# Written order on four engines for the three chains of attention units, and one load on another engine's queue

## The chip, the cores and the metric

The kernel is one launch on one core of a Trainium2 chip. The time is the device time of that launch in microseconds; three runs are shown with their median. One more execution was taken with the hardware profiler on, and everything that is read from a trace comes from it. Engines are named as in the profile: PE is TensorE (PEld its weight loads), DVE is VectorE, ACT is ScalarE, POOL is GpSimd, SP is SyncE, which issues most of the DMAs.

## The reference, cut to what matters

The program is a decoder of four layers on `x`, 4 sequences of 256 tokens of width 128, with a second input `ctx`, 4 sequences of 512 keys. Layers 0, 1 and 3 have multi-head attention with 16 heads of 8; in outline:

```python
# layer 0
x = x + self_attention(norm(x))                    # 16 heads of 8, keys are x's own 256 rows
x = x + cross_attention(norm(x), norm(ctx), mask)  # 512 keys, with a key mask
x = x + moe(norm(x))                               # 32 experts, best 1, and a shared expert
# layer 1
x = x + causal_self_attention(norm(x))
x = x + strided_cross_attention(norm(x), norm(ctx))  # keys are every 16th row of ctx
x = x + moe(norm(x))                               # 8 experts, best 2
# layer 2: linear attention, latent attention, moe
# layer 3
x = x + latent_self_attention(norm(x))             # queries and keys through a narrow product
x = x + cross_attention(norm(x), ctx)              # 512 keys, an additive mask
x = x + quantised_ffn(norm(x))                     # rows rounded to integer steps, GELU, rounded again
```

Each normalisation is a layer norm over 128 columns. The router of a mixture takes the logits of the normalised rows, chooses the experts, and computes for each token its rank within its expert.

## The kernel before, in words

**Units.** `woven` runs the attention of one layer as a chain of *units*. A unit is one sequence in one kind of attention: layer 0 has units 0 to 3 (self, 256 keys) and 4 to 7 (cross, 512 keys), layer 1 has four, layer 3 has units 0 to 3 (latent) and 4 to 7 (cross). A unit is made of small steps:

- its *prelude*: `norm` (statistics on VectorE, L309; then on GpSimd `ve` L314, a power, and the normalised rows, `xn` or `xq`, L322), `source` (the rows turned by TensorE, L332, evicted as `xnT`, L292), in layer 3's first half the latent product (L941), then `queries` (L463 to L503) and `keys` (L512 to L526). In units 0 and 1 queries and keys stay on the chip; from unit 2 on in layers 0 and 3 each is split into three bf16 parts, written to DRAM (`qp`, `kp`) and read back in another arrangement (L497, L526) by DMAs on SP's queue. In layer 0 these land in a part of the tile `e0h` that is lent to them; in layer 3 in `cn`, `w2kv`, `kk` and `qq`.
- *beats*: half of a group of row scores (L564 or L582, with the row maximum on VectorE, L571 or L575) and half of a group of column scores (L643, L656 or L679, with the exponential on ScalarE, L673). Row maxima of one unit are made while the columns of the unit before are. The PSUM ring of scores has 7 buffers; one beat takes 4.
- *late* steps: `weighted` (L701, eight matmuls for half a group), `divided_by_sums`, `transposed_result`, `added`, and after them `u.after`, a list of further steps spread over `u.within` of a unit. In layer 0's units 4 to 7 and in all of layer 1 that list ends with the router's steps (in layer 1 the strided attention's stand ahead of them); in layer 3's units 4 to 7 it is the quantised feed-forward (`quantised_steps`): `norm`, `quantise` (its first instruction is the reduction `am`, L2154), `turn`, `hidden` (two products, then GELU on ScalarE, L2187), `quantise_hidden` (L2154 again), two `turn_hidden`, `result`.
- *beside*: steps of other work that are spread over the unit. In layer 0's units 0 to 3 these are the means and scales of the context; in unit 0 a fourth one is `loads`, the first half of layer 0's expert weights (`e0h`, four DMAs of 1 MB, L2282).

**The written order.** Every step carries a place within the unit, as a fraction. `back` gives the beats and late steps, `front` the preludes of units n + 1, n + 2 and n + 3 and the steps beside; `run` sorts by the fraction and calls them. What lies at 1.0 or later is carried into the next unit.

**What sets the order of execution.** The framework keeps each instruction's data dependencies. Where the code isn't inside `tc.manual_schedule`, its planner chooses the order of the instructions on every engine, by its own idea of when each could start. Two other loops of the kernel (the expert blocks of layer 0's mixture, and the linear attention) run inside `tc.manual_schedule` already: there the engines named keep the order in which the code issues. `woven` did not. [...]DMAs are issued in order of the queue of the engine that issues them; here these are SP, ACT and, for the gathers, POOL.

At layer 3's start the tokens of layer 2's mixture are still being fetched: `back` (L1372, an indirect DMA on POOL's queue), and VectorE adds them to `x` (L1384) ahead of each unit's `norm`. Layer 3's constant parts of the keys and queries (`restk`, `restq`, L463) are written into DRAM early, during layer 0.

Of the kernel before, what the change touches and what calls it, by code (L numbers as in the profile page):

```python
# [203 lines left out]
def decoder(ctx: ExitStack, tc: tile.TileContext, dr, out):  # L204
    nc = tc.nc
    V, A, G, T = nc.vector, nc.scalar, nc.gpsimd, nc.tensor
# [79 lines left out]
    turn = [0]  # L286
# [9 lines left out]
    def normalise(srcs, dsts, on=None):  # L296

        scaled_by(statistics(srcs), srcs, dsts, on)
# [94 lines left out]
    def spread(fns, start, end):  # L393

        n = len(fns)
        return [(start + (end - start) * (i + 0.5) / n, f) for i, f in enumerate(fns)]

    def call(f, *args):
        return lambda *more: f(*args, *more)
# [32 lines left out]
    def woven(pool, units, n_keys, split=None, lent=None):  # L432
# [312 lines left out]
        def prelude(u):  # L745
            return [call(f, u) for f in u.prelude] + [call(queries, u), call(keys, u)]

        def groups_of_rows(u):
            if u.clip:
                return []  # L750
            return [call(rows_of, u, qt, g) for qt in range(2) for g in range(0, 4, 512 // u.nk)]
# [19 lines left out]
        def halved(groups):  # L771
            return [(f, h) for f in groups for h in range(2)]
# [22 lines left out]
        LEAD = 2  # L795
# [53 lines left out]
        def run(items):  # L849
            for _, f in sorted(items, key=lambda i: i[0]):  # L850
                f()
# [1 line left out]
        for n, u in enumerate(units):  # L853
            u.n, u.split = n, bool(split) and n > 1
        halves_of_rows = [halved(groups_of_rows(u)) for u in units]
        for f in prelude(units[0]) + [call(values, units[0])]:
            f()
        first = []
        if len(units) > 1:
            first += spread(prelude(units[1]), 0.0, 0.8)  # L860
        first += beats([], halves_of_rows[0] + halves_of_rows[1][:LEAD], units[0])[0]
        run(first)
        carried = []
        for n in range(len(units)):
            own, late = back(n)
            items = own + front(n) + carried + late
            run([i for i in items if i[0] < 1.0])
            following = 1.0
            if n + 1 < len(units):
                following = units[n].nkt / units[n + 1].nkt  # L870
            carried = [((at - 1.0) * following, f) for at, f in items if at >= 1.0]
        run(carried)

    def scaled(pool, bias):
        t = pool.tile([P, 1], F32, tag="qb", name="qb", bufs=2)
# [110 lines left out]
            spare.pop(0)(tag)  # L986

    class Router:  # L990

# [15 lines left out]
        def steps(r, pool, b, tag):  # L1007
            n_e, k = r.n_e, r.k
            mine = slice(2 * k * b, 2 * k * (b + 1))
            u = {}  # L1010
# [93 lines left out]
                else:  # L1104
                    V.tensor_copy(r.seen, total)

            out = [norm, turn, logits]
            if r.probs:
                out.append(softmax)
            out.append(choose)  # L1110
# [1033 lines left out]
    def quantised_steps(pool, b):  # L2144


        wq, ws = wq3
        u = {}

        def quantised(src, m, tag):  # L2150


            am = small.tile([P, 2], F32, tag="am", name="am")
            V.tensor_reduce(am, src, AX.X, ALU.max, apply_absolute_value=True)  # L2154
            V.tensor_scalar(am, am, EPS, None, ALU.max)
            sc = small.tile([P, 2], F32, tag="qs", name="qs")
            V.reciprocal(sc, am)
            V.tensor_scalar(sc, sc, 127.0, None, ALU.mult)
            un = small.tile([P, 2], F32, tag="un", name="un")
            V.reciprocal(un, sc)  # L2160
            V.tensor_scalar(un, un, ws[:, m : m + 1], None, ALU.mult)
            q = pool.tile(list(src.shape), F32, tag=tag, name=tag)
            for i in range(2):
                V.tensor_scalar(q[:, i], src[:, i], sc[:, i : i + 1], MAGIC, ALU.mult, ALU.add)
            V.tensor_scalar(q, q, MAGIC + 127.0, MAGIC - 128.0, ALU.min, ALU.max)
            return q, un

        def norm():
            two = [x[2 * b], x[2 * b + 1]]
            u["xn"] = pool.tile([P, 2, D], F32, tag="xq", name="xq")  # L2170
            normalise(two, [u["xn"][:, i] for i in range(2)], G)

        def quantise():
            u["q"], u["un"] = quantised(u["xn"], 0, "q1")

        def turn():
            u["qT"] = pool.tile([P, S], BF16, tag="qT1", name="qT1")
            transposed(
                [u["q"][:, i] for i in range(2)], u["qT"],
                lambda d, s: V.tensor_scalar(d, s, MAGIC, None, ALU.subtract), tag="s1",  # L2180
            )

        def hidden():
            hp = [product(u["qT"][:, i * P : (i + 1) * P], wq[0], "s1") for i in range(2)]
            u["h"] = pool.tile([P, 2, 512], F32, tag="h", name="h")
            for i in range(2):
                A.activation(u["h"][:, i], hp[i], AF.Gelu, scale=u["un"][:, i : i + 1])  # L2187

        def quantise_hidden():
            u["qh"], u["unh"] = quantised(u["h"], 1, "q4")  # L2190
            u["qhT"] = pool.tile([P, 2, 512], BF16, tag="qT4", name="qT4")

        def turn_hidden(i):
            transposed(
                [u["qh"][:, i, c * P : (c + 1) * P] for c in range(4)], u["qhT"][:, i],
                lambda d, s: A.activation(d, s, AF.Copy, bias=-MAGIC), tag="s1",
            )

        def result():
            y = ps("s1")  # L2200
            for i in range(2):
                for c in range(4):
                    T.matmul(
                        y[:, i * P : (i + 1) * P], lhsT=u["qhT"][:, i, c * P : (c + 1) * P],
                        rhs=wq[1][:, c * P : (c + 1) * P], start=c == 0, stop=c == 3,
                    )
            for i in range(2):
                t = 2 * b + i
                V.scalar_tensor_tensor(
                    x[t], y[:, i * P : (i + 1) * P], u["unh"][:, i : i + 1], x[t], ALU.mult, ALU.add  # L2210
                )
                nc.sync.dma_start(out[t * P : (t + 1) * P, :], x[t])

        return [
            norm, quantise, turn, hidden, quantise_hidden, call(turn_hidden, 0),
            call(turn_hidden, 1), result,
        ]

# [51 lines left out]
    def layer_0(wh, router):  # L2270
        with ExitStack() as st:
            st.enter_context(psum_pool("ps0"))
            pool = attn_pool(st, "l0")


            lent = Lent(wh[:, 16 * 512 :])
            neg0, neg0T = key_mask(pool, "mbk0", False, lent)

            def loads():
                for i in range(0, 16, 4):  # L2280
                    cols = slice(i * 512, (i + 4) * 512)
                    nc.sync.dma_start(wh[:, cols], dr["e0h"][:, cols])  # L2282

            units = self_units(pool, w0a, True, False, 0)
            units += cross_units(
                pool, w0x, 2, context_T,
                row_mask=lambda b: neg0[:, b * SK : (b + 1) * SK],
                key_bias=lambda b: lambda kt: neg0T[:, NKT * b + kt : NKT * b + kt + 1],
            )
            for u in units[:B]:  # L2290
                u.beside = [call(context_means, u.b, 0), call(context_means, u.b, 2)]
                u.beside += [call(context_scales, u.b)]
            units[0].beside += [loads]
            for u in units[B:]:
                u.beside = [call(normalise_context, u.b, i) for i in range(0, NKT, 2)]
                u.after, u.within = router.steps(pool, u.b, "s1"), 1.0
            woven(pool, units, SK, "l0", lent)
# [17 lines left out]
    def layer_3():  # L2315
        with ExitStack() as st:
            st.enter_context(psum_pool("ps3"))
            pool = attn_pool(st, "l3")
            mc, mcT = (added_mask(pool, k, 2, True) for k in ("mcau", "mcauT"))
            mf, mfT = added_mask(pool, "mif1", 2, False), added_mask(pool, "mif1T", NKT, False)  # L2320
            units = low_rank_units(
                pool, w3a, rows_mask=lambda qt: mc[:, qt, :], cols_mask=lambda kt: mcT[:, kt, :]
            )
            units += cross_units(
                pool, w3x, 10, lambda b: None, rows_mask=lambda b: lambda qt: mf[:, qt, :],
                cols_mask=lambda b: lambda kt: mfT[:, kt, :],
            )
            for u in units[B:]:
                u.after, u.within = quantised_steps(pool, u.b), 0.8
            lent = Lent(cn.rearrange("p t d -> p (t d)"), held["w2kv"])  # L2330
            woven(pool, units, SK, "l3", lent)

    with early:
        e0h = e0.tile([P, 32 * 512], F32, tag="e0h", name="e0h")
# [4 lines left out]
    late = ctx.enter_context(tc.tile_pool(name="late", bufs=1, reuse_waits="tile"))  # L2339
# [39 lines left out]
```

## Time and profile before

| what | value |
|---|---|
| three runs | 1522.98, 1516.32, 1518.51 us; median 1518.51 |
| profiled execution | 1517.87 us |
| its span | 1516.0 us, mean granted TensorE clock 0.912 |
| layer 0's attention | 7 to 282 us of the span |
| layer 1's attention | 336 to 472 |
| layer 3 | 1180 to 1516 |
| DMA | 95.85 MB, mean 63 GB/s |

A row of waits reads: engine, tile and line that waited, `<-`, what it waited for, then total us, number of times, longest one. A row of the timeline reads: start, duration, engine, line, operation, output and input, shapes, and in brackets how long the engine had been idle just before, and what ended that. `SPq` is SP issuing a DMA; the duration is that of the issue. In the page, a digit of the row PEclk is the granted TensorE clock in tenths for one fortieth of the span.

Layer 2, the mixtures and the loads between (282 to 336, 472 to 1180) are not part of `woven`.

### The profile page before, as it was taken

The page shows a single profiled execution, that of the slowest core. Times are in us where ns is not written, and L with a number is a line of the kernel's source. Part 1 is how long each engine was busy: PE and PEld are TensorE (multiplying, and loading weights), DVE is VectorE, ACT ScalarE, POOL GpSimd, SP SyncE. Part 2 cuts the span into 40 slices and gives each one's busy share as a digit, 9 for nine tenths or more (in the row PEclk, how much of TensorE's full clock was granted, in tenths as well). Part 3 has the DMA queues.
Part 4 walks back from the last instruction along what each step waited for, and adds up shares of the span by engine and source line. Part 5 has one row for each costly group of instructions (what it writes and reads, how often), then busy time and mean ns, then how long its engine had stood idle before and what let it go on. Part 6 is the DMA issues. An engine that isn't in the chain of part 4 may idle for free.

```text
span 1516.0 us, 29457 instructions
## 1 busy us (share of the span) xinstructions
PE 1292.0 (85%) x11200; PEld 709.5 (47%) x11200; DVE 821.6 (54%) x2696; ACT 722.7 (48%) x1462; POOL 324.1 (21%) x481
## 2 busy tenths in 40 slices
PE   4878999796787998879999999999597489898894
PEld 2434454343354664535555555555365244443442
DVE  6368785485654346555445445452333456776643
ACT  0343667285542334257767757756121024345464
POOL 6133221344123316000000000000331613322000
PEclk9699999896897999999999999999698579999997
DMA  3432120620132115230111000000312112221000
GB/s 137 171 101 89 62 66 6 239 55 14 62 157 87 41 34 208 83 120 15 56 46 43 1 5 1 1 4 1 128 39 56 35 50 78 95 62 62 6 5 8
DMA packets 50873, 95.85 MB, mean 63 GB/s; under 512 B 6881, under 2 KB 31947, under 8 KB 49067
## 3 DMA queue, kind: packets, MB, share of 16 engines
q1 hardware_dynamic: 46318, 77.61, 14.8%
q0 software_dynamic: 3264, 6.69, 2.0%
q10 hardware_dynamic: 1152, 9.67, 1.6%
q8 instruction: 90, 1.47, 0.4%
q14 instruction: 49, 0.40, 0.1%
HBM read 66.20 MB, written 29.72 MB: 63 GB/s over the span
## 4 chain that ended last, share of the span: by engine, by line
PE 62%; DVE 10%; ACT 8%; DMA 7%; POOL 7%; issue 5%; SPq 1%; ACTq 0%; POOLq 0%; DVEq 0%
PE o L2040 6%; PE g L1299 6%; PE o L701 5%; PE s L2020 5%; PE f L1966 4%; PE s L582 4%; PE y L1323 3%; PE s L679 3%; PE f L1952 2%; PE s L643 2%; DMA e0h<-kp 2%; DVE mx L571 2%; PE s L656 2%; PE t L1308 2%; PE s L2013 2%
## 5 line engine op out<-in xcount | busy, mean ns | idle before, releaser
L673 ACT ACTIVATE pr<-s 128x512 f32<-128x512 f32 x384 | 206.4, 597 | 254.1 <-PE s L679 160.4
L314 POOL TENSOR_SCALAR ve<-mv 128x2 f32<-128x2 f32 x44 | 10.7, 243 | 743.6 <-DVE mv L309 738.6
L1977 ACT ACTIVATE ss<-ss,ntop 128x768 f32<-128x768 f32 x128 | 118.6, 928 | 91.1 <-DVE ntop L1975 90.9
L571 DVE TENSOR_REDUCE mx<-s 128x1 f32<-128x512 f32 (+1 forms) x192 | 122.5, 684 | 61.8 <-PE s L656 25.3
L701 PE MATMUL o<-pr,v 128*32 128x256 f32 (+1 forms) x1792 | 146.2, 396 | 7.5 <-ACT os L707 6.0
L1971 DVE CUSTOM_DVE_ANT_0 ss<-f,n 128x512 f32<-128x512 f32 x128 | 83.5, 689 | 68.7 <-PE f L1966 68.7
L2040 PE MATMUL o<-pr,v 128*64 128x256 f32 x768 | 107.5, 395 | 1.0 <-ACT pr L2027 0.9
L575 DVE CUSTOM_DVE_ANT_0 junk<-s,nmif 128x512 bf16<-128x512 f32 x128 | 82.9, 688 | 36.0 <-PE s L679 35.5
L2020 PE MATMUL s<-qT,kT 64*128 64x256 f32 x768 | 101.5, 381 | 0.0
L2027 ACT ACTIVATE pr<-s,n 128x512 f32<-128x512 f32 x128 | 80.3, 678 | 24.4 <-PE s L2020 24.2
L582 PE MATMUL s<-e0h 32*128 32x512 bf16 (+1 forms) x576 | 73.0, 365 | 18.8 <-DMA e0h<-kp 18.3
L1277 POOL DMA_INDIRECT xb<-sent,token x62 | 60.0, 968 | 105.7 <-PE t L1284 59.0
L1966 PE MATMUL f<-kT,qT 64*128 64x512 f32 x256 | 78.1, 629 | 2.2 <-ACT kT L294 1.1
L1959 DVE CUSTOM_DVE_ANT_0 ss<-f,nought 128x256 f32<-128x256 f32 x128 | 46.7, 421 | 54.6 <-PE f L1952 53.1
L2040 PEld LDWEIGHTS o<-pr,v 128*64 128x64 f32 x768 | 47.8, 137 | 57.3 <-issue 22.7
L701 PEld LDWEIGHTS o<-pr,v 128*32 128x32 f32 x1792 | 40.1, 110 | 70.6 <-issue 46.4
L679 PE MATMUL s<-e0h 32*128 32x256 bf16 x960 | 68.4, 273 | 3.6 <-DVE mx L571 2.2
L2020 PEld LDWEIGHTS s<-qT,kT 64*128 64x128 f32 x768 | 67.8, 190 | 6.0
L656 PE MATMUL s<-qm,kc 32*128 32x512 f32 (+1 forms) x256 | 64.3, 710 | 0.0
L575 DVE CUSTOM_DVE_ANT_0 junk<-s,nmcau 128x256 bf16<-128x256 f32 x128 | 46.2, 421 | 32.9 <-PE s L656 15.0
L332 PE MATMUL s<-consts,xn 128*128 128x128 f32 x64 | 20.2, 371 | 46.0 <-POOL xn L322 46.0
L322 POOL TENSOR_SCALAR xn<-x,mv,rs 128x128 f32<-128x128 f32 x72 | 56.8, 797 | 3.8
(482 smaller groups left out, 2663.2 us busy)
## 6 DMA issues: line engine op xcount, KB each, us to landing
qp<-qp SPq DMA_DIRECT2D x36, 192.0 KB, 2.3
kd<-ahead SPq DMA_DIRECT2D x20, 256.0 KB, 2.6
vd<-ahead SPq DMA_DIRECT2D x20, 256.0 KB
kT<-kd SPq DMA_DIRECT2D x20, 256.0 KB, 4.9
v<-vd SPq DMA_DIRECT2D x5, 1024.0 KB, 5.3
e0h<-qp SPq DMA_DIRECT2D x6, 768.0 KB
e0h<-in_e0h SPq DMA_DIRECT2D x4, 1024.0 KB, 12.0
e0h<-in_e0h SPq DMA_DIRECT2D x1, 4096.0 KB
```

What stands on the lines that cost most here:

```text
L571: V.tensor_reduce(u.mx[:, qt, j, g : g + per], sc, AX.X, ALU.max)
L575: V.tensor_tensor_reduce(junk[:, : u.nk], sc[:, i, :], u.rows_mask(qt), 1.0, -3e38, ALU.add, ALU.max, accum_out=u.mx[:, qt, j, g + i : g + ...
L582: T.matmul(sc[:, i, :], lhsT=u.q3[r, g + i, c, qt * P : (qt + 1) * P], rhs=u.kk[r, g + i, : u.nk], start=n == 0, stop=n == 3 * per - 1,)
L656: T.matmul(sc, lhsT=u.kc[r, kt * P : (kt + 1) * P], rhs=u.qm[r, gp : gp + 2, first:], start=u.clip, stop=True,)
L673: A.activation(dst, sc, AF.Exp)
L679: T.matmul(sc[:, i, :], lhsT=u.kk[r, gp + i, kt * P : (kt + 1) * P], rhs=u.q3[r, gp + i, c, :], start=u.cols_mask is None and n == 0, stop ...
L701: T.matmul(u.po[gp][32 * j : 32 * j + 32, i, first:], lhsT=u.v[:, kt, 4 * j + gp + i, :], rhs=u.pr[gp, kt, j][:, i, first:], start=kt + i ...
L1299: T.matmul(p[r], lhsT=xbT[b][:, r], rhs=w(512 * i), start=biases is None, stop=True,)
L1966: T.matmul(sc[h], lhsT=qT[u, c][hrow[h], qt * P : (qt + 1) * P], rhs=kT[u, c][hrow[h], :SK], start=True, stop=True,)
L1977: A.activation(ss[qt][h], ss[qt][h], AF.Exp, bias=ntop[:, qt, h, c : c + 1], accum_out=total[:, qt, h, c : c + 1],)
L2020: T.matmul(sc[h][:, i, :], lhsT=kT[u, c][hrow[h], kt * P : (kt + 1) * P], rhs=qT[u, c][hrow[h], :], start=False, stop=i == 1,)
L2040: T.matmul(po[u, g][hrow[h], i, :], lhsT=v[u][:, kt, n * hd : (n + 1) * hd], rhs=pr[u, g, kt, h][:, i, :], start=kt + i == 0, stop=kt + i ...
```

## The change

Three edits:

1. The body of `woven` (the first unit's prelude, the opening row groups, the loop over the units and the carried tail) goes inside `tc.manual_schedule` with VectorE, ScalarE, TensorE and GpSimd in the set. On these four, instructions keep the written order, in layers 0, 1 and 3. SP is not in the set.
2. A step `rest` that does nothing stands after `norm` in the router's list and in the quantised feed-forward's list, so that one slot lies between `norm` and the step after it. In layer 3 `within` goes from 0.8 to 0.9, so that the slots keep their length there; layer 0 has 1.0 over one slot more, and layer 1's `within` grows with the list. Layer 2's latent attention uses the router too, and its steps are spread anew.
3. Layer 0's `loads` go from SP's queue to ScalarE's, and `keep_in_program_order` ties each DMA to its place in the written order, which is 0.875 of unit 0.

```diff
@@ woven
-        for f in prelude(units[0]) + [call(values, units[0])]:
-            f()
...
-        run(carried)
+        by_hand = {mybir.EngineType.DVE, mybir.EngineType.Activation, mybir.EngineType.PE}
+        by_hand.add(mybir.EngineType.Pool)
+        with tc.manual_schedule(engines=by_hand):
+            for f in prelude(units[0]) + [call(values, units[0])]:
+                f()
...
+            for n in range(len(units)):
+                own, late = back(n)
+                items = own + front(n) + carried + late
+                run([i for i in items if i[0] < 1.0])
...
+            run(carried)
@@
+    def rest():
+        pass
@@ Router.steps
-            out = [norm, turn, logits]
+            out = [norm, rest, turn, logits]
@@ quantised_steps
-            norm, quantise, turn, hidden, quantise_hidden, call(turn_hidden, 0),
+            norm, rest, quantise, turn, hidden, quantise_hidden, call(turn_hidden, 0),
@@ layer_0, loads
-                    nc.sync.dma_start(wh[:, cols], dr["e0h"][:, cols])
+                    tc.keep_in_program_order(A.dma_start(wh[:, cols], dr["e0h"][:, cols]))
@@ layer_3
-                u.after, u.within = quantised_steps(pool, u.b), 0.8
+                u.after, u.within = quantised_steps(pool, u.b), 0.9
```

More of the change, by code (lines that the diff above doesn't have):

```diff
@@ L855, in woven @@
         halves_of_rows = [halved(groups_of_rows(u)) for u in units]
-        for f in prelude(units[0]) + [call(values, units[0])]:
-            f()
[L858 to L871, printed above, removed]
-        run(carried)
+        by_hand = {mybir.EngineType.DVE, mybir.EngineType.Activation, mybir.EngineType.PE}
[3 more added lines that the diff above has]
+                f()
+            first = []
+            if len(units) > 1:
+                first += spread(prelude(units[1]), 0.0, 0.8)
+            first += beats([], halves_of_rows[0] + halves_of_rows[1][:LEAD], units[0])[0]
+            run(first)
+            carried = []
+            for n in range(len(units)):
+                own, late = back(n)
+                items = own + front(n) + carried + late
+                run([i for i in items if i[0] < 1.0])
+                following = 1.0
+                if n + 1 < len(units):
+                    following = units[n].nkt / units[n + 1].nkt
+                carried = [((at - 1.0) * following, f) for at, f in items if at >= 1.0]
+            run(carried)
     def scaled(pool, bias):
```

## The prediction

> **What bounds the kernel now.** I read the page first (busy shares, slices, chain), then the busy times of the three stages that the change touches, then the waits, and last the timeline around every wait of over 2 us.
>
> ```profile
> span 1516.0 us, 29457 instructions
> PE 1292.0 (85%) x11200; PEld 709.5 (47%) x11200; DVE 821.6 (54%) x2696; ACT 722.7 (48%) x1462; POOL 324.1 (21%) x481
> PEclk9699999896897999999999999999698579999997
> ```
> ```profile
> 7.00:282.00 275.00, 224.32 (x2876) 118.32 (x2876) 177.19 (x478) 124.89 (x245) 85.03 (x136) 0.91 0.28 99
> 336.00:472.00 136.00, 101.55 (x764) 59.38 (x756) 77.72 (x243) 66.10 (x147) 41.82 (x65) 0.83 0.18 70
> 1180.00:1516.00 336.00, 274.31 (x3100) 130.21 (x3100) 194.77 (x775) 139.86 (x258) 78.92 (x118) 0.87 0.14 44
> ```
>
> The second fence is busy time in layer 0's, layer 1's and layer 3's attention (stretch, length, then PE, PEld, DVE, ACT, POOL, clock). TensorE sets the pace. It is idle for 51, 34 and 62 us in them, and the clock row dips where it is. Only those idle times, and the half-clock work behind them, can be won: the change removes no arithmetic. The waits that matter:
>
> ```profile
> PE s L582 <- DMA e0h<-kp: 18.3, 4, 5.5
> PE s L582 <- DVE mx L575: 12.2, 8, 4.0
> DVE am L2154 <- POOL xq L322: 12.1, 4, 3.6
> ```
> ```profile
> DVE x L1384 <- DMA back<-done,index: 7.9, 4, 3.0
> PE s L941 <- DVE xnT L292: 6.4, 2, 5.9
> ```
>
> The last two are the waits of 1180 to 1262 alone. I went through the order in which TensorE ran its groups against the order in which `woven` writes them, in all three stages. TensorE already runs the written order, apart from two places in layer 0. So the change acts through VectorE, ScalarE and GpSimd, where the planner did move work.
>
> **Term A: layer 3's second half, −9 us.** From the timeline:
>
> ```profile
> 1382.67 0.42 DVE L2154 TENSOR_REDUCE am<-xq 128x2 f32<-128x256 f32 x1 [3.64 <-POOL xq L322]
> 1384.35 0.37 PE L582 MATMUL s<-cn,w2kv 32*128 32x512 bf16 x1 [3.97 <-DVE mx L575]
> ...
> 1428.21 0.42 DVE L2154 TENSOR_REDUCE am<-xq 128x2 f32<-128x256 f32 x1 [2.84 <-POOL xq L322]
> 1430.41 0.58 PE L582 MATMUL s<-cn,qq 32*128 32x512 bf16 x1 [3.50 <-DVE mx L575]
> ```
>
> Reader, see how one wait makes the next: the planner put `quantise`'s first reduction directly behind the norm; VectorE stood for 3.64 and 2.84 us until GpSimd had the normalised rows; the row maxima behind it were late; no score buffer came free, and TensorE stood for 3.97 and 3.50. In the written order, `norm`, `rest` and `quantise` lie slots apart, with about three beats of 2.0 to 2.2 us between norm and quantise. GpSimd's part is 0.23 (L314), about 0.7 for the power, 1.58 (L322) and the gaps between: some 3.6 us, less than two beats. Both waits go: 7.5 us of TensorE.
>
> The clock goes with them. After the two gaps beats and weighted sums ran at about half rate (groups of eight at 1.08 instead of 0.64, a beat at 2.43 instead of 1.37): 1.5 and 2.9 us more than full rate. The Trainium skill's "TensorE: Matmul & The Clock Gate", Part 1, has the clock drop after an idle window of about 3.4 us and come back after one window of sustained work; half a window would be lost, 1.7 per gap, 3.4 in all against the trace's 4.4. I take the trace's, which also shows half rate for some 4 us behind a gap of only 2.46 us (at 180). Gross gain 11.9.
>
> What is late next: VectorE's own work. `quantise` is a burst of about 2.3 us, and a beat leaves only about 0.7 of VectorE free (2.1 less 1.38 of row reads), so the reads behind it come some 1.5 late; two buffers of slack take part of that. I charge 1.5 for each of the two units: −9. `quantise_hidden` waits for ScalarE's GELU either way ("DVE am L2154 <- ACT h L2187: 14.0, 4, 7.0"): one unit gets a beat more between the two, the other a beat less: 0. Bounds −12 (no burst felt) to −2 (every burst delays a beat fully and takes the clock).
>
> **Term B: layer 3's start, −4 us.**
>
> ```profile
> 1209.32 0.35 DVE L1384 SCALAR_TENSOR_TENSOR x<-back,best,x 128x128 f32<-128x128 f32 x1 [3.05 <-DMA back<-done,index]
> 1211.78 0.35 DVE L1384 SCALAR_TENSOR_TENSOR x<-back,best,x 128x128 f32<-128x128 f32 x1 [2.12 <-DMA back<-done,index]
> ```
>
> VectorE stands at the fetched expert rows, because the planner raised those adds above row reads that were ready. In the written order they come later, when the rows are there. Against it: GpSimd's queue in written order does unit 0's shared query copies (3.6 us) and two fetches' four issues (4 x 1.25 = 5.0) ahead of unit 1's power and normalisation, so unit 1's rows come at about 1197 instead of 1186; the latent product that needs them was at 1198.9 and would be at 1198.5: a tie. Unit 2's would come at 1218.7 instead of 1223.8. I take −4; bounds −6 (all 7.9 but two) and +5 (the tie lost by one fetch).
>
> **Term C: layer 0's chain and loads, −2 us.**
>
> ```profile
> 53.14 0.59 SPq L2282 DMA_DIRECT2D e0h<-in_e0h  x1
> 53.91 0.34 SPq L497 DMA_DIRECT2D e0h<-qp  x1
> 54.52 0.57 SPq L526 DMA_DIRECT2D e0h<-kp  x1
> 55.15 1.77 SPq L2282 DMA_DIRECT2D e0h<-in_e0h  x3
> ...
> 79.56 0.74 SPq L463 DMA_DIRECT2D qp<-in_restq  x1
> 80.47 0.35 SPq L497 DMA_DIRECT2D e0h<-qp  x1
> 80.93 0.56 SPq L526 DMA_DIRECT2D e0h<-kp  x1
> ```
> ```profile
> 61.11 0.37 PE L582 MATMUL s<-e0h 32*128 32x256 bf16 x1 [5.08 <-DMA e0h<-kp]
> 92.57 0.37 PE L582 MATMUL s<-e0h 32*128 32x256 bf16 x1 [5.26 <-DMA e0h<-kp]
> ```
>
> SP's queue: the first megabyte of expert weights is ahead of unit 2's keys, which took 6.54 us to land; the third load of keys, with nothing beside it, took 4.70 (112.84). The second took 11.51, but it stands behind layer 3's `in_restq`, not behind the weights. SP is not in the manual set, so nothing fixes that one. On ScalarE's queue the loads stand behind unit 0's exponentials and issue at about 61 to 63: the first gap is then about 3 us shorter (6.54 towards 4.70, and the load itself off the queue ahead). ScalarE pays 4 issues of about 0.5 (six like them took 3 us at 410): 2 us, beside TensorE's beats, and with an exponential due in each beat I charge 0.5.
>
> Here a rule speaks against the change: "DMA: Bandwidth & Descriptors", section "Issuing engines are not separate DMA queues": another issuing engine saves issue time only, the 16 DMA engines are shared. In the trace the four megabytes moved from 54 to 69, 15 us; shifted, they run to about 78, into unit 3's key and query writes (75 to 80). By the queue reading the first gap loses 3; by the rule the load takes the same share from unit 3 and gives the 3 back. I keep −3 and charge 1 for the overlap.
>
> Lost: at the gaps at 61 and 92 the planner had drawn a group of eight weighted sums ahead of the blocked beat, inside the gap (0.64 full, 1.07 half rate, two groups): now they come after: +1 to +2 each if the gap stays, about +2 for both with the first one short. Clock won by the shorter first gap: behind 61.11 four beats took 14.6 instead of about 10; a third of 4.6 is −1.5. Sum: −3 + 1 + 0.5 + 2 − 1.5 = −1; if `in_restq` happens to move off unit 3's keys (SP is planned anew, an even chance) the second gap gives 2 more on the mean: −2 to −3; I take −2. Bounds −9 (both gaps shortened to 2) and +12.
>
> **Term D: layer 1, and the rest.** Orders equal, tail too; `rest` moves the router's turn by one slot, which hides one norm: −1 to 0, I take −0.5 (bounds −2, +3, its tail being a chain). `rest` in layer 0 and in the latent router shifts steps by under a beat where TensorE is 95% busy: 0, bounds ±1.
>
> Sum: −9 − 4 − 2 − 0.5 = −15.5 on the profiled execution's 1517.87 gives 1502.4; the median of the runs shown is 0.6 above it. Predicted: 1503.
>
> **The rivals.**
> *R1, the expected waits change their name* (chance 0.2): bursts on VectorE in fixed order delay row reads as the waits did, and the lost freedom elsewhere eats the rest; A is −3, B 0, C +2: about 1517. For it: VectorE is the only engine with under 0.7 us free per beat. Against it: the idle rows name a producer (GpSimd) that will be done, not VectorE's own work.
> *R2, one term of A and B only* (0.15): −6, 1512.
> *R3, the strict order holds beats behind late keys in layer 0* (0.2): the loads on ScalarE start at 62, collide with unit 3's writes, which already queue behind `in_restq`: the keys come 6 us later than now, with 2 of clock, the hoisted groups' 4 are lost, ScalarE's issues cost 2: +14. From the point where A and B bring under 6 the kernel is slower: 1518 + 14 − 5 = 1527. For it: the second gap's landing of 11.51. Against it: packets of the weights were through in 15 us.
> *R4, nothing changes*, since TensorE is already in the written order: inside R1.
>
> **How the numbers follow.** No difference under 0.5% (7.6 us) can be told here from no change. The main case (0.45) runs 1494 to 1510; R2 straddles the lower bound, 1511; R1 lies within; R3 is past the upper one, 1526. Faster: the main case and half of R2, 0.52. Same: R1 and the other half of R2, 0.28. Slower: R3, 0.20. The range runs from 1490 (A and C at their good ends) to 1525, leaving R3's upper half out.
>
> **What would show it.** Right: no VectorE wait at L2154 for L322 over 1 us; no TensorE gap of 3 us at 1380 and 1426; VectorE idle before L1384 under 1 us; loads on ScalarE's queue at 61 to 65; a clock of layer 3 above 0.87. Wrong: a wait of L582 for keys above 18.3 us, gaps of layer 0 at 75 to 95 that are longer, TensorE waiting for row maxima (L575) behind `quantise` or the norms, or for `xn` (L322) at 1190 to 1200.

## The result, and the profile after

The changed kernel takes 1497.71 us (median; 1494.47 to 1498.68) where the kernel before took 1517.41 beside it (1514.14 to 1522.98): ratio 0.9863, 95% interval 0.9829 to 0.9896. Run again later, in another comparison, it was 0.9902 (0.9865 to 0.9939). The gain is clear of noise; its size is 15 to 21 us. The profiled execution took 1498.68 us, its span 1496.8.

From the page of the changed kernel, and its busy times in the stretches of layer 0, layer 1 and layer 3 (columns as before the change: stretch, length, PE, PEld, DVE, ACT, POOL, clock):

```profile
span 1496.8 us, 29470 instructions
PE 1276.3 (85%) x11199; PEld 701.0 (47%) x11200; DVE 831.4 (56%) x2696; ACT 722.8 (48%) x1462; POOL 324.4 (22%) x481
PEclk8899999897897999989999999999879669999997
```
```profile
7.00:270.00 263.00, 215.10 (x2874) 113.42 (x2875) 180.80 (x475) 125.35 (x246) 84.96 (x134) 0.92 0.29 104
334.00:467.00 133.00, 95.08 (x693) 54.47 (x693) 74.33 (x231) 59.93 (x131) 38.06 (x61) 0.81 0.17 68
1180.00:1496.80 316.80, 262.38 (x3099) 125.18 (x3100) 198.55 (x778) 139.97 (x258) 79.25 (x119) 0.90 0.15 46
```

Layer 3 is 19 us shorter at about the same place on the time line: TensorE's idle time in it went from 62 to 54 us, and its busy time from 274 to 262, for the same instructions. The second part goes with the clock (0.87 to 0.90). Layer 0 is 12 us shorter. The row of layer 1 (133 us for 136) is not a gain: its window began 13 us ahead of layer 1's first normalised rows before and 3 us ahead of them now; the table below goes by marks. The waits (line numbers below `woven` are now 4 to 7 higher: L945 was L941, L1391 was L1384, L2161 was L2154):

```profile
PE s L582 <- DMA e0h<-kp: 15.1, 4, 6.1
DVE am L2161 <- POOL xq L322: 5.7, 2, 2.8
```

The second row was 12.1 in 4 waits. The two that are left, 2.83 us each, are those of units 6 and 7, when the last row maxima have been made and none can come late behind them. "PE s L582 <- DVE mx L575", 12.2 before, is gone from layer 3's second half. Keys are still waited for.

**Where the time went, stretch by stretch.** The marks are instructions that every version has: the evictions of results (L707, two for each unit), the first normalised rows (L322) of layers 1 and 3, and, as the end, the last but one store of `out_x`, about 3 us ahead of the end of the span. Lengths in us, one profiled execution each:

| stretch | before | changed | changed again |
|---|---|---|---|
| start to unit 0's first result | 54.3 | 50.5 | 51.5 |
| from there to unit 1's second result | 49.6 | 38.8 | 39.4 |
| rest of layer 0's units | 166.1 | 169.2 | 172.1 |
| layer 0's mixture, to layer 1's first normalised rows | 79.3 | 78.7 | 80.8 |
| from there to layer 1's first result | 24.3 | 27.9 | 28.6 |
| rest of layer 1's units | 65.5 | 69.1 | 65.4 |
| layer 1's last result to layer 3's first normalised rows | 740.7 | 746.4 | 750.8 |
| from there to unit 3's last result | 151.9 | 144.1 | 145.9 |
| unit 4 | 39.0 | 39.4 | 39.4 |
| from unit 4's last result to the end | 142.1 | 129.6 | 131.1 |

So 30 to 36 us were won, nearly all in four stretches, and 16 to 22 lost in the others. Some of the losses are in stretches that the change hardly touches; they are taken up below.

### The profile page after: what moved, and what is told of

Same layout as the page of the kernel before. It is cut to its first block, busy times and chain, and to the rows that moved or that the text cites. A ratio compares the mean times of both kernels' runs of the same rounds, so it can differ in the third digit from the quotient of the medians.

```text
span 1496.8 us, 29470 instructions
## 1 busy us (share of the span) xinstructions
PE 1276.3 (85%) x11199; PEld 701.0 (47%) x11200; DVE 831.4 (56%) x2696; ACT 722.8 (48%) x1462; POOL 324.4 (22%) x481
## 4 chain that ended last, share of the span: by engine, by line
PE 63%; DVE 12%; ACT 7%; POOL 7%; DMA 5%; issue 5%; SPq 1%; ACTq 0%; POOLq 0%; DVEq 0%
PE o L2047 6%; PE g L1306 6%; PE o L701 5%; PE s L2027 5%; PE f L1973 4%; PE s L582 4%; PE y L1330 3%; PE s L679 3%; PE f L1959 2%; PE s L643 2%; DVE mx L571 2%; PE s L364 2%; PE s L656 2%; PE t L1315 2%; POOL back L1379 2%
## 5 line engine op out<-in xcount | busy, mean ns | idle before, releaser
L575 DVE CUSTOM_DVE_ANT_0 junk<-s,nmif 128x512 bf16<-128x512 f32 x128 | 82.8, 687 | 32.3 <-PE s L679 31.6
L582 PE MATMUL s<-e0h 32*128 32x512 bf16 (+1 forms) x576 | 70.4, 354 | 15.6 <-DMA e0h<-kp 15.1
L1284 POOL DMA_INDIRECT xb<-sent,token x62 | 60.3, 972 | 103.6 <-PE t L1291 58.7
L1973 PE MATMUL f<-kT,qT 64*128 64x512 f32 x256 | 79.3, 647 | 2.3 <-ACT kT L294 1.1
L575 DVE CUSTOM_DVE_ANT_0 junk<-s,nmcau 128x256 bf16<-128x256 f32 x128 | 46.1, 421 | 28.8 <-PE s L656 12.5
L656 PE MATMUL s<-qm,kc 32*128 32x512 f32 (+1 forms) x256 | 59.5, 674 | 0.0
L322 POOL TENSOR_SCALAR xn<-x,mv,rs 128x128 f32<-128x128 f32 x72 | 57.9, 811 | 3.8
```

Source lines behind the costliest of these rows:

```text
L575: V.tensor_tensor_reduce(junk[:, : u.nk], sc[:, i, :], u.rows_mask(qt), 1.0, -3e38, ALU.add, ALU.max, accum_out=u.mx[:, qt, j, g + i : g + ...
L582: T.matmul(sc[:, i, :], lhsT=u.q3[r, g + i, c, qt * P : (qt + 1) * P], rhs=u.kk[r, g + i, : u.nk], start=n == 0, stop=n == 3 * per - 1,)
L656: T.matmul(sc, lhsT=u.kc[r, kt * P : (kt + 1) * P], rhs=u.qm[r, gp : gp + 2, first:], start=u.clip, stop=True,)
L1973: T.matmul(sc[h], lhsT=qT[u, c][hrow[h], qt * P : (qt + 1) * P], rhs=kT[u, c][hrow[h], :SK], start=True, stop=True,)
```

## The experiments

Twelve kernels, one of them twice, with ratios to the kernel before, each measured beside its own runs of it. The stretches are those of the table; "units 0, 1" is the start to unit 1's second result (103.9 before), "l3 start" is layer 3's first normalised rows to unit 3's last result (151.9), "l3 second half" is unit 4's last result to the end (142.1).

| kernel | ratio (interval) | units 0, 1 | l3 start | l3 second half |
|---|---|---|---|---|
| changed | 0.9863 (0.9829 to 0.9896) | 89.2 | 144.1 | 129.6 |
| changed again | 0.9902 (0.9865 to 0.9939) | 90.9 | 145.9 | 131.1 |
| changed, loads on SP | 0.9946 (0.9931 to 0.9962) | 99.7 | 145.7 | 131.1 |
| the same, `in_restq` late | 0.9902 (0.9883 to 0.9922) | 93.2 | 143.1 | 131.1 |
| before, loads on ScalarE | 0.9943 (0.9926 to 0.9960) | 94.1 | 150.8 | 145.1 |
| changed, no empty step | 0.9968 (0.9949 to 0.9987) | 91.0 | 142.9 | 141.2 |
| empty step alone | 1.0003 (0.9984 to 1.0022) | 103.4 | 150.4 | 142.3 |
| layer 3's part alone | 0.9889 (0.9870 to 0.9909) | 101.7 | 147.3 | 131.1 |
| changed, GpSimd planned | 0.9919 (0.9895 to 0.9943) | 94.0 | 144.3 | 129.6 |
| changed, layer 1 planned | 0.9868 (0.9820 to 0.9915) | 87.5 | 143.3 | 131.1 |
| changed, layer 1's norm early | 0.9843 (0.9800 to 0.9886) | 89.5 | 143.9 | 130.1 |
| changed, keys early | 0.9812 (0.9776 to 0.9847) | 88.5 | 140.3 | 130.1 |
| three edits together | 0.9844 (0.9809 to 0.9879) | 87.5 | 140.6 | 131.0 |

**The loads: which queue, and why it matters.** One edit each way, against the changed kernel and against the kernel before:

```diff
-                    tc.keep_in_program_order(A.dma_start(wh[:, cols], dr["e0h"][:, cols]))
+                    nc.sync.dma_start(wh[:, cols], dr["e0h"][:, cols])
```

> The changed kernel with layer 0's four weight loads back on SP's queue; written order and the empty step stay. Theory: the large gain in layer 0 (8 us between unit 1's first and second result) is not the weights' own traffic but what their leaving SP does to SP's order: with the loads on SP, layer 3's in_restq is again issued ahead of unit 3's keys, those land some 11 us after their issue instead of about 4.5, and TensorE stands about 5 us at that beat, with half clock behind it. Expected: 6 to 10 us slower than the changed kernel, about 1505; opening, layer 1 and layer 3 as in the changed kernel. Rival (the gain in layer 0 comes from the written order of the four engines): within 2 us of the changed kernel, 1498, and the second wait for keys stays under 2 us.

And the opposite edit in the kernel before:

> The kernel before with only the four weight loads moved to ScalarE's queue in program order. Theory: the first two waits for keys in layer 0 get shorter, the second from 5.3 to under 2 us, since in_restq falls behind unit 3's keys; 6 to 10 us faster than before, about 1509, all of it won before 105 us of the span; the opening's 4.8 us wait for GpSimd's query copies stays, layers 1 and 3 stay. Rival (issuing engine does not matter, the 16 DMA engines are shared, the load costs the same at unit 3): within 2 us of before, 1517.

Measured: the loads back on SP cost the changed kernel most of layer 0's gain (0.9946; units 0 and 1 back to 99.7). The move alone, with everything else planned, is worth 0.9943, 8.7 us on the median of 1521.96 beside it, and units 0 and 1 take 9.8 us less. Both theories held in their direction, and both rivals fell. In size the second one held (6 to 10 us). The first was too mild: the second wait for keys is 8.55 us where about 5 were expected, and the ratio is 0.4 to 0.8% above the changed kernel's, 7 to 13 us for the 6 to 10. What happened on SP, from the timeline with the loads on SP:

```profile
74.44 0.74 SPq L463 DMA_DIRECT2D qp<-in_restq  x1
75.34 0.35 SPq L497 DMA_DIRECT2D e0h<-qp  x1
75.80 0.56 SPq L526 DMA_DIRECT2D e0h<-kp  x1
...
87.89 0.37 PE L582 MATMUL s<-e0h 32*128 32x256 bf16 x1 [8.55 <-DMA e0h<-kp]
```

and from that of the changed kernel:

```profile
75.42 0.56 SPq L526 DMA_DIRECT2D e0h<-kp  x1
76.04 0.78 SPq L463 DMA_DIRECT2D qp<-in_restq  x1
...
79.94 0.26 PE L582 MATMUL s<-e0h 32*128 32x256 bf16 x1 [1.38 <-DMA e0h<-kp]
```

The same key load, issued within 0.4 us of the same time: 12 us to its use in one, 4.5 in the other. What changed places just there is layer 3's `in_restq`, which the planner issues in front of the keys when the weights are on SP, and behind them when they are not. The DMA records say how it holds the keys up. The keys are 512 packets of 512 bytes, `in_restq` 96 packets of 6 KB. With `in_restq` in front, 416 of the key packets had moved by 80.2 us; from there to 85.9 the DMA engines moved 72 packets of 6 KB and none of 512 bytes, at a busy share of 18.5% of the 16 engines, about what three of them would give; then the last 96 key packets, three sixteenths, followed. That these 96 stood behind `in_restq` on the same three engines is an inference from these shares. With `in_restq` behind, all of the key packets had moved by 79.4. To part `in_restq` from the weights, both were put where they can't be confused: weights on SP, and layer 3's two constant loads kept at their written place in layer 3.

```diff
-                nc.sync.dma_start(
+                tc.keep_in_program_order(nc.sync.dma_start(
                     t.bitcast(I32)[:, :, 3], r.unsqueeze(0).to_broadcast([3, 32, r.shape[1]])
-                )
+                ))
```

> As the run with layer 0's weight loads back on SP's queue (written order and empty step kept), but layer 3's in_restk and in_restq are kept at their written place, at layer 3's start, so they are no longer issued in layer 0. Theory: what made unit 3's keys late in layer 0 is in_restq ahead of them on SP, not the weights; with the weights still on SP the second wait for keys falls from about 5 us to under 2, and layer 0 up to unit 1's second result is 8 to 10 us shorter than with in_restq there: total about 8 us under the run with the loads on SP, 0.989 of before. Rival (the weights' own traffic, or SP being busy with them, makes the keys late): the second wait stays at about 5 us and the total at 0.995.

Measured 0.9902, units 0 and 1 at 93.2: of the 10.4 us between 99.7 and the changed kernel's 89.2, 6.5 go with the two constant loads, though the weights are still on SP (8 to 10 had been expected). The second wait for keys is 3.19 us, neither under 2 nor 5: here SP issued these keys at 79.09 instead of 75.42, because the planner put the query load ahead of the keys' own writes. The other 4 us are not shown to belong to the weights: the other kernels in written order with the weights on ScalarE have 87.5 to 94.0 in these two units. Traffic, order on SP and what one execution differs from another are not told apart there.

The Trainium skill says in "DMA: Bandwidth & Descriptors", section "Issuing engines are not separate DMA queues", that another issuing engine saves issue time only. As to the transfers nothing here speaks against it. But the edit also changed what the queue left behind issues first: the whole move is worth 8.7 us by the runs, where the issue time of the four loads on SP is 2.4.

**The empty step, with and without the written order.**

```diff
-            out = [norm, rest, turn, logits]
+            out = [norm, turn, logits]
...
-            norm, rest, quantise, turn, hidden, quantise_hidden, call(turn_hidden, 0),
+            norm, quantise, turn, hidden, quantise_hidden, call(turn_hidden, 0),
...
-                u.after, u.within = quantised_steps(pool, u.b), 0.9
+                u.after, u.within = quantised_steps(pool, u.b), 0.8
```

> The changed kernel without the empty step in both lists, layer 3's within at 0.8 again; written order and loads as changed. Theory: in written order norm and quantise are then one slot apart, about 2 beats instead of 3 to 4; GpSimd's part of 3.6 us still fits, so layer 3 keeps nearly all of its gain: 0 to 3 us slower than the changed kernel there, and layer 2, whose router loses the empty step again, wins back up to 6. Total 1492 to 1501. Rival (the empty step is what frees VectorE): VectorE waits 2 to 4 us for xq at units 4 and 5 again, 8 to 12 us slower, about 1508.

And the reverse, the empty step and 0.9 with no `manual_schedule` in `woven` and the loads on SP:

> The empty step and within 0.9 alone: the planner orders all three chains, the loads stay on SP. Theory: where norm stands in the written list hardly binds the planner; it draws quantise's first reduction behind the norm again, VectorE waits about 3 us for xq at units 4 and 5, and the kernel is within 4 us of before, 1518 to 1522 where before is 1522. Rival (the slot is what counts, whoever keeps the order): the two waits go, layer 3's second half is 8 to 12 us shorter, total about 1511.

Measured: without the empty step 0.9968, and layer 3's second half is 141.2, as before the change. My theory had it the other way round, and fell; the rival's time came true, but not the wait that it named, as the rows below show. The empty step alone is worth nothing: 1.0003, second half 142.3, and the two waits are there to the hundredth. From the timeline of the empty step alone:

```profile
1394.40 0.42 DVE L2161 TENSOR_REDUCE am<-xq 128x2 f32<-128x256 f32 x1 [3.64 <-POOL xq L322]
1396.08 0.58 PE L582 MATMUL s<-cn,w2kv 32*128 32x512 bf16 x1 [3.97 <-DVE mx L575]
```

From the written order without the empty step, unit 4:

```profile
1380.61 1.58 POOL L322 TENSOR_SCALAR xq<-x,mv,rs 128x128 f32<-128x128 f32 x2
1383.29 0.42 DVE L2161 TENSOR_REDUCE am<-xq 128x2 f32<-128x256 f32 x1
1386.79 0.41 PE L332 MATMUL s<-consts,q 128*128 128x128 f32 x2 [2.31 <-DVE q L2172]
```

From the changed kernel, the same unit:

```profile
1375.56 1.58 POOL L322 TENSOR_SCALAR xq<-x,mv,rs 128x128 f32<-128x128 f32 x2
1380.11 0.42 DVE L2161 TENSOR_REDUCE am<-xq 128x2 f32<-128x256 f32 x1
1383.89 0.44 PE L332 MATMUL s<-consts,q 128*128 128x128 f32 x2
```

This is the row to read. In written order VectorE waits for GpSimd at unit 4 in neither (at unit 5 its reduction still stands 1.66 us without the step, and TensorE 2.69 behind it). But GpSimd's rows are done 1.1 us before `am` without the step and 3.0 with it, and without it the wait shows one engine further: TensorE stands 2.31 us at the turn of the quantised rows. With the step there is no wait at either place. The waits for GELU at `quantise_hidden` follow too: before, VectorE stood in four of them for 14.0 us; written order alone leaves 9.0 in two, order and step 2.0 in one. From unit 4's last result to near the end TensorE is busy for 109.7 us without the step (clock 0.90) and 105.1 with it (0.94). Slot and order are each worth next to nothing in this stretch, and together 11 to 12.5 us: all ten profiles with both have 129.6 to 131.1, before and the three that lack one of them or both 141.2 to 145.1. (On the way the written order alone was up to 4.8 us ahead of before, at unit 6's first result, and lost that again by the end.)

**Layer 3 alone.** `manual_schedule` only where `split == "l3"`, the empty step only in `quantised_steps`, loads on SP:

```diff
-        with tc.manual_schedule(engines=by_hand):
+        with tc.manual_schedule(engines=by_hand) if split == "l3" else nullcontext():
...
-            out = [norm, rest, turn, logits]
+            out = [norm, turn, logits]
...
-                    tc.keep_in_program_order(A.dma_start(wh[:, cols], dr["e0h"][:, cols]))
+                    nc.sync.dma_start(wh[:, cols], dr["e0h"][:, cols])
```

> Written order and the empty step in layer 3 alone; layers 0 and 1 planned, the loads on SP. Theory: layer 3's gains do not depend on the rest: 6 to 8 at its start and 11 to 12 in its second half, 17 to 20 us shorter from layer 3's first normalised row to the end than before; total 0.988. Rival (what is won in layer 3 depends on what the stages before it leave): under 12.

Measured 0.9889 (0.9870 to 0.9909): nearly as much as the whole change. From layer 3's first normalised rows to the end it is 15.1 us shorter than before (4.6 at the start, 11.0 in the second half, and 0.4 longer in unit 4), less than the 17 to 20 that I expected. Added to the loads' 0.57%, these 1.11% make 1.68; the changed kernel has 1.37 and 0.98. If the two parts add, the written order in layers 0 and 1, with the router's empty step, costs on balance some 5 to 11 us; that is an estimate, and its lower end lies inside the intervals. The stretches say where: behind unit 1's result layer 0's units take 169 to 172 us against 166 (kernels with the planner and no empty step: 165.99 to 166.90), and layer 1's opening 28 against 24.

**GpSimd out of the set.**

```diff
-        by_hand.add(mybir.EngineType.Pool)
```

> The changed kernel with GpSimd out of the set of engines in written order. Theory: the planner raises later units' norms on GpSimd ahead of unit 0's query copies (L503) in layer 0's opening again, TensorE stands 4.8 us there, 3 to 4 us are lost at the first result; at layer 3's second half GpSimd has only the norms, so its gain of 11 to 12 us stays; total 3 to 6 us over the changed kernel, 0.992. Rival (VectorE's order already fixes when the norms' statistics are there, so GpSimd cannot run them early): no difference.

Measured 0.9919, above both ratios of the changed kernel, but its interval overlaps theirs: not told apart. (Units 0 and 1 took 94.0; 2 of the 3 to 5 us more are a second wait for keys of 3.31 instead of 1.38, the load taking 5.49 us.) Unit 0's first result comes at 51.4, as in the changed kernel, and the 4.83 us wait for the query copies is gone here too. As to the opening the rival was right: it is won by VectorE's order, which makes the later units' statistics late, so that GpSimd has nothing to draw forward.

**Layer 1.** First, its chain left to the planner (`if split else nullcontext()`):

> The changed kernel with layer 1's chain left to the planner (no manual schedule there), the rest as changed. Theory: written order costs layer 1 about 6.5 us (3.6 in its opening, where unit 1's norm waits on VectorE behind the eviction of unit 0's values, and 3 behind it); the planner takes that back: about 6 us faster than the changed kernel, 1492. Rival (layer 1 is a chain and its 6.5 us come from the empty step in the router or from the clock): within 2 us of the changed kernel.

Then unit 1's norm written ahead of unit 0's values:

```diff
-            for f in prelude(units[0]) + [call(values, units[0])]:
+            ahead = [] if split else prelude(units[1])[:1]
+            for f in prelude(units[0]) + ahead + [call(values, units[0])]:
                 f()
...
-                first += spread(prelude(units[1]), 0.0, 0.8)
+                first += spread(prelude(units[1])[len(ahead) :], 0.0, 0.8)
```

> The changed kernel with unit 1's norm written ahead of unit 0's values in layer 1's opening (only there), so that VectorE does its statistics before it waits for TensorE's values. Theory: the 3.6 us that the opening lost come back: layer 1's first result 3 us earlier against the start of layer 1, total 2 to 4 us under the changed kernel. Rival (layer 1 is a chain bound elsewhere and what comes early waits later): the first result comes earlier, the last one does not, total within 1.5 us.

Measured: planned, the opening is 24.5 us, as before; with the norm early 23.1. Both theories of the opening held in the traces. In the changed kernel one sees VectorE at the head of its queue with a step that isn't ready, for 3.02 us, and unit 1's additions and statistics held behind it:

```profile
342.67 0.42 DVE L540 COPY v<-s 128x256 f32<-128x256 f32 x1 [3.02 <-PE s L533]
343.01 0.48 DVE L1389 TENSOR_TENSOR x<-x,back 128x128 f32<-128x128 f32 x2
343.41 0.29 DVE L308 BATCH_NORM_STATS2 st<-x 128x6 f32<-128x128 f32 x1
```

The totals, 0.9868 and 0.9843, can't be told from the changed kernel's. The rest of layer 1 is 64.9 to 66.6 us in eight of the thirteen profiles, the second one of the changed kernel among them, and 68.2 to 69.2 in five, the first one of the changed kernel among these. Since one kernel stands in both groups, the 3.6 us there are not shown to be of the change.

**The changed kernel again.**

> The changed kernel as it is, on the chip and in the minutes of the three beside it, so that these are compared with it and not with a run of another day. Expected: 0.984 to 0.989 of before. What it tells besides: the stretch of layer 2, which the change hardly touches, took 6 us more in the changed kernel's profiled run than in that of before; if that is a property of the change it is there again, if it is what one execution differs from another it moves by several us.

Measured 0.9902, above the 0.984 to 0.989 that I expected, and its profile has a span of 1508.4, 11.6 us more than the first one of the same kernel. Layer 2's stretch is 750.8. It was 747.3 in the kernel with only the loads moved, which issues layer 2's instructions in the order of before on every engine. So executions with one order there differ by 4 to 7 us in that stretch, and the 5.7 us that the change "lost" there in the first pair of profiles are not shown to be its own. The same holds for layer 0's mixture (78.7 to 85.0).

**Keys earlier, and three edits together.**

```diff
-                    end = 0.35 if units[n].nk < SK else 0.5
+                    end = 0.2 if units[n].nk < SK else 0.5
```

> The changed kernel with the preludes of split units spread over the first 0.2 instead of 0.35 of a unit of 256 keys, so that keys and queries start on their way through DRAM about 2 to 3 us earlier. Theory: the waits for keys that are left in layer 0 (6.1 and 5.6 us in the changed kernel) and at layer 3's start (2.5 and 3.1) shrink by 2 us each, 4 to 8 us faster than the changed kernel. Rival (the packed prelude delays beats by as much, on ScalarE and GpSimd): the same within 2 us, with waits for keys shorter and waits for row maxima or exponentials longer.

The last kernel has this, the early norm of layer 1 and the constants kept in layer 3:

> The changed kernel with three more edits: preludes of split units over 0.2 instead of 0.35, unit 1's norm ahead of unit 0's values in layer 1, and layer 3's in_restk and in_restq kept at their written place. Theory: the waits for keys of layers 0 and 3 get shorter by 1 to 2 us each and nothing new becomes late: 0.980 to 0.984 of before, 5 to 10 us under the changed kernel. Rival (what the edits win is given back in the following beats, or in_restq at layer 3's start delays the fetch of the experts' rows): 0.986 to 0.990, as the changed kernel.

Measured: the first wait for keys falls from 6.14 to 2.73 us, the third from 5.58 to 3.48, and layer 3's start is 140.3 instead of 144 to 146. The ratio is 0.9812; the changed kernel beside it had 0.9902, and the two intervals do not touch, but against the changed kernel's other ratio they do. The three edits together have 0.9844: nothing beyond the keys' edit is shown. Both beat the kernel before; that the early keys beat the changed kernel is shown by one of two comparisons and by the stretches, about 5 us.

## Why the prediction was right or wrong

The time forecast was 1503, the measured 1497.7, and the sign and mechanism in layer 3 came as written. But the sum is nearer than its terms, and that is in part luck: in the first profile the terms A, B and C were forecast 3.5, 3.8 and 9.6 us too small, layer 1 came out 7.7 worse than forecast, and another 5.5 were lost in stretches where they are not shown to be of the change.

**Term A (forecast −9).** Measured −12.5 and −11. The order and the slot did what the working says: both VectorE waits of units 4 and 5 and both TensorE waits are gone. (Those of VectorE at units 6 and 7 stayed, against the sign that I had named.) From unit 4's last result to the last instruction TensorE's idle time fell from 30.2 us to 24.8 in both profiles of the changed kernel, 5.4 where the forecast had 4.5 (7.5 for the two gaps, less 3 for the bursts). Its busy time fell from 112.1 to 105.1 and 106.6, at a clock of 0.91 and then 0.94 and 0.93. So the term that was mis-sized most is the clock: 5.5 to 7.1 us for the 4.4 that the trace's count gave; the estimate from the rule of the Trainium skill ("TensorE: Matmul & The Clock Gate", Part 1), 3.4, was further off. It is no clean test of either, since the stretch also lost smaller gaps. Among these are three of 1.3 to 1.5 us for row maxima behind the waits for GELU, which I had put at nothing. The burst was charged a little too much: of TensorE's waits for row maxima there one of 1.75 us is all over 1 us that came:

```profile
1398.04 0.66 PE L332 MATMUL s<-consts,q 128*128 128x128 f32 x4 [1.75 <-DVE mx L575]
```

What I had not seen is that the order wins nothing here without the slot; my own expectation after the result still held the slot for a detail.

**Term B (forecast −4).** Measured −7.8 and −6.0. The working by queues held to within half a microsecond. Unit 1's latent product is a tie, forecast at 1198.5 and at 1198.90 in both kernels. TensorE stood 5.89 us there for `xnT` before and now stands 5.03 for `xn`, one of the signs that I had named for being wrong; the wait has changed its name and kept most of its cost. Unit 2's was forecast at 1218.7. Before, and then in the changed kernel:

```profile
1198.90 1.11 PE L941 MATMUL s<-xnT,w3a 128*64 128x256 f32 x2 [5.89 <-DVE xnT L292]
```
```profile
1197.13 0.48 PE L332 MATMUL s<-consts,xn 128*128 128x128 f32 x1 [5.03 <-POOL xn L322]
...
1217.09 0.47 PE L332 MATMUL s<-consts,xn 128*128 128x128 f32 x1 [1.84 <-POOL xn L322]
...
1218.80 1.12 PE L945 MATMUL s<-xnT,w3a 128*64 128x256 f32 x2 [0.46 <-ACT xnT L294]
```

VectorE's waits for the fetched rows, 7.9 us before, are gone, and with them a wait of TensorE behind them in the kernel before, which I had not listed:

```profile
1212.88 2.76 PE L564 MATMUL s<-kc,qm 32*128 32x256 f32 x12 [4.78 <-DVE mx L575]
```

Layer 3's first result is 5.8 and 5.9 us nearer to its first normalised rows than before, and up to 2 us more followed by unit 3's last. The term was too small because it counted no clock: TensorE's idle time to unit 3's last result fell by 3.3 and 3.9 us, which is the forecast, and its busy time by another 4.5 and 2.1, at a clock of 0.84 and 0.82 for 0.80.

**Term C (forecast −2).** Measured −14.7 and −13.0 by unit 1's second result, −11.6 and −7.0 by the end of layer 0's units. Three steps failed. First, the opening: I had gone through TensorE's order, and not through what GpSimd did in the first 20 us. There the planner had drawn later units' normalised rows ahead of unit 0's query copies, which is term A's mechanism in another place. Before, and then in the changed kernel:

```profile
15.20 1.58 POOL L322 TENSOR_SCALAR xn<-x,mv,rs 128x128 f32<-128x128 f32 x2
19.23 3.63 POOL L503 TENSOR_SCALAR qm<-q,consts 128x256 f32<-128x256 f32 x4
20.22 2.13 PE L564 MATMUL s<-kc,qm 32*128 32x256 f32 x16 [4.83 <-POOL qm L503]
```
```profile
14.13 3.62 POOL L503 TENSOR_SCALAR qm<-q,consts 128x256 f32<-128x256 f32 x4 [2.05 <-ACT q L491]
15.16 3.98 PE L564 MATMUL s<-kc,qm 32*128 32x256 f32 x32
```

Second, "`in_restq` happens to move off unit 3's keys, an even chance": it was the first thing to go, and it goes with the loads in both orders of the rest. With `in_restk` it was worth 6.5 us in the one kernel that parts it from the weights, three times the 2 us that I gave it on the mean. Third, the first wait for keys did not get 3 us shorter: it is 6.14 for 5.08, because TensorE came 6 us earlier to that beat and the keys only 5. The overlap of the weights with unit 3's keys (R3's mechanism, and the rule's) did not show: those keys took 4.38 us. (The loads went out at 58.7 to 60.8, a little ahead of the forecast 61 to 65.) The clock of that stretch went from 0.76 to 0.91.

**Term D (forecast −0.5).** Measured +4 in layer 1's opening, shown by the two kernels that take it back. I had compared TensorE's order, which is indeed the same; the loss is in VectorE's, in the one place where written order puts a step that waits ahead of steps that are ready. And "0, bounds ±1" for layer 0 was too low: of the 3 to 6 us that its units behind unit 1 lost, units 4 to 7 have 1.3 in one profile and 3.0 in the other, units 2 and 3 the rest. The empty step alone, with the planner, also has 169.2 us behind unit 1, so the step has a part in it, and order without it 171.9.

**The rivals.** R1 (the waits change their name) is what the written order without the empty step does: nothing won in layer 3's second half. R2 (one term alone) did not come, R3's conditions did not come about, and R4 stood inside R1.

## What to carry to other kernels

Where a planner orders and an engine waits at the head of its queue for a producer that is nearly done, look at what the planner put there too early: fixing the order and leaving a slot for the producer belong together, and here each alone was worth nothing in that stretch. Go through every engine's order, not only that of the engine that sets the pace. When a transfer is moved to another queue, read what the queue it left issues next: here 6.5 of the 10.4 us in layer 0's first two units went with other loads that no longer stood in front of the keys. And take one profile of the same kernel twice before a few microseconds of an untouched stretch are explained.

## What the runs showed of the hardware that I had not expected

A key load of 256 KB that takes 4.4 us from issue took 11.5 and 12.0 when `in_restq`, 576 KB in packets of 6 KB, was issued 1.4 us ahead of it on the same queue, in both orders of the rest of the kernel. The 16 DMA engines were busy for 18.5% on the mean while the last 96 key packets had yet to move, so the engines together had time to spare. Behind a gap of TensorE of only 2.46 us, before the change, the granted clock was 0.50 for 3.4 us (180.1 to 183.5); around the gap of 5.08 us, from 56.0 to 61.1, it was 0.50 from 57.3 to 74.2. Two executions of one kernel differed by 11.6 us in span: 2.9 in layer 0's later units, 2.1 in its mixture, 4.4 between layer 1's last result and layer 3's first normalised rows, the rest spread out, at mean clocks of 0.917 and 0.910.
